# Layer norms transposed by VectorE and a trip through DRAM instead of by TensorE, in a two-layer graph-attention kernel

**Chip, cores, metric.** One core of one Trainium2 chip. The metric is the device time of one execution in microseconds (us), the median of several runs of the built kernel. A ratio is the mean time of one kernel's fast runs over the mean of the other's in the same rounds, so it is not quite the ratio of the medians that stand beside it; its 95% interval follows in brackets.

## The reference, cut to what matters

```python
# x: [64, 256, 512] fp32 (64 batches of 256 nodes), adj: [256, 256]
h = relu(layernorm(x));  x = x + L0(h, adj)      # W: 512x256; softmax over neighbours; concat [out, h W]
h = relu(layernorm(x));  x = x + L1(h, adj)      # q, k, v, o: 512x512 each, with bias; 8 heads of 64, masked softmax
```

Both layers multiply `h` by weights. The kernel's matmuls take `h` with its 512 features on partitions (the axis that the product `h W` sums over), while its layer norms have the nodes on partitions. Each normed 128x512 tile therefore has to be transposed before its product: 4 tiles per group (2 batches) and layer, 256 tiles in all. How this is done is the subject of the change.

## The kernel before

The kernel works by groups of two batches. While TensorE does the attention of group g, it also does the projection (q, k, v) of group g+1 and the first layer of group g+2, piece by piece, in an order that the program fixes. A projection is seven block products in two PSUM banks; each bank is read by ScalarE (`kept`) or VectorE (the additions) before it is accumulated into further. The other engines' orders are chosen when the program is built, except where `after` fixes one.

```python
def after(instruction, name):            # same engine: stand behind `name`; no semaphore is waited for
    tc.add_manual_dep(instruction.ins, name, ...NoSync...)

def norm_T(src, mv, name):               # src [128, 4 tiles, 512]
    ve = small.tile([P, GT], F32, ...);   nc.vector.tensor_scalar(ve, mv[:, :, 1], EPS, None, op0=ALU.add)
    rstd = small.tile([P, GT], F32, ...); nc.gpsimd.tensor_tensor(rstd, ve, rexp, op=ALU.pow)
    def normed(t):
        xn[t] = att.tile([P, D], F32, tag="xn", ..., bufs=2)          # two buffers
        nc.vector.tensor_scalar(xn[t], src[:, t, :], mv[:, t, 0:1], rstd[:, t : t + 1], ...)
    def put(t, dst):
        if t + 1 < GT: normed(t + 1)
        pt = mm(...)                                                   # a PSUM bank
        for c in range(HP): transpose(pt[:, c, :], xn[t][:, c * P : (c + 1) * P], ident)   # TensorE
        nc.scalar.activation(dst, pt, AF.Relu)
    normed(0)
    return put

def operand_sums(quads, sums):            # GpSimd; used for the projection (sums) and for the outputs (o_sums)
    a11, a12, a21, a22 = quads
    nc.gpsimd.tensor_add(sums[:, 0], a21, a22)
    nc.gpsimd.tensor_sub(sums[:, 1], sums[:, 0], a11)
    nc.gpsimd.tensor_sub(sums[:, 2], a11, a21)
    nc.gpsimd.tensor_sub(sums[:, 3], a12, sums[:, 1])

# project(g), for name in q, k, v   (cut to banks and readers)
    def kept(bank, half, i):
        s = att.tile([P, 2, N], F32, tag=f"kept{i}", ..., bufs=1);  take(s, bank, half);  return s
    product(first, 1, True);   p1 = kept(first, 0, 0)
    product(second, 2, True);  nc.vector.tensor_add(part(0, 0), second, p1)
    product(first, 6, False);  p16 = kept(first, 0, 1)
    second = ...               # another bank
    product(second, 7, True);  p7 = kept(second, 1, 2)
    product(first, 5, False);  nc.vector.tensor_add(part(1, 1), first, p7)
    product(second, 4, False); nc.vector.tensor_add(part(1, 0), second, p16)
    product(first, 3, False);  take(part(0, 1), first, 1)   # may start only when the addition from `first` is done

# outputs(g, b): o_sums (GpSimd), seven products of half size, after each: nc.vector.tensor_add(x, out, x)
# weigh(...): attention-weighted sums (pr), reciprocal of the totals, oT; scores(...): sc, exp (ScalarE), mask product (VectorE)
# judge(): a bound on the scores from the weights, checked in small pieces between the others
```

## Time and profile before

| | before |
|---|---|
| time, median of 4 runs (lowest to highest) | 2700.3 us (2698.2 to 2701.9) |
| mean granted TensorE clock | 0.993 |
| busy: TensorE / VectorE / GpSimd / ScalarE | 97 / 62 / 46 / 31% |
| period of a group in mid-kernel | 81.54 us |
| TensorE's waits between 100 and 2600 us | 27 us |

The period is the distance between the same VectorE addition (the first one for `k`) in neighbouring groups, in the timeline. The busy shares, waits, timeline and groups of this kernel are shown in the prediction below.

### The profile page before, as it was taken

Reading aid. Unit: us, or ns where it says so; the run is one execution under the profiler, and the core shown is the slowest. Engines: PE = TensorE matmul, PEld = TensorE weight load, DVE = VectorE, ACT = ScalarE, POOL = GpSimd, SP = SyncE. Lnnn points to the kernel's source line nnn. Section 1 sums busy time; section 2 is a strip of 40 time slices with the busy share of each in tenths; the row PEclk is TensorE's granted clock in tenths of the full one; section 3 lists DMA queues with packets and bytes.
Section 4 is the critical chain, followed back from the end, with each engine's and each line's share of the span. In section 5 each row is a group of like instructions: output and inputs, shape, how many; then the busy total and the mean of one; then the engine's idle time right before and its main releaser. Section 6 shows DMA issues by size and latency. Waiting matters only on the chain.

```text
span 2697.3 us, 41512 instructions
## 1 busy us (share of the span) xinstructions
PE 2620.4 (97%) x17150; PEld 2118.8 (79%) x17150; DVE 1669.7 (62%) x2558; ACT 835.9 (31%) x1771; POOL 1230.0 (46%) x1004
## 2 busy tenths in 40 slices
PE   5999999999999999999999999999999999999997
PEld 3888888878888887887788888788878878878874
DVE  5666566666557665566665576665576656666544
ACT  2333232333332333323333323333333333233321
POOL 2353355443445443545434454435455335445343
PEclk8999999999999999999999999999999999999998
DMA  5000101000001010000000000000000000000000
GB/s 164 1 12 32 36 24 36 13 32 32 28 32 36 9 36 32 24 32 9 32 32 24 32 32 9 32 32 24 32 32 9 32 32 24 32 17 23 17 16 25
DMA packets 45890, 78.49 MB, mean 29 GB/s; under 512 B 3712, under 2 KB 10624, under 8 KB 45696
## 3 DMA queue, kind: packets, MB, share of 16 engines
q1 hardware_dynamic: 45696, 75.77, 8.1%
q8 instruction: 137, 2.24, 0.3%
q14 instruction: 57, 0.47, 0.1%
HBM read 42.21 MB, written 33.55 MB: 28 GB/s over the span
## 4 chain that ended last, share of the span: by engine, by line
PE 89%; DVE 8%; POOL 1%; issue 1%; DMA 0%; ACT 0%; DVEq 0%
PE pq L113 15%; PE pv L113 14%; PE py L113 13%; PE pk L113 13%; PE pr L113 9%; PE ph L113 8%; PE sc L113 7%; PE po L113 4%; PE pt L116 4%; DVE p L573 3%; DVE r L604 2%; PE total L113 2%; DVE k L544 1%; DVE oT L605 1%; PE pn L116 1%
## 5 line engine op out<-in xcount | busy, mean ns | idle before, releaser
L573 DVE TENSOR_TENSOR p<-p,maskT 128x1024 f32<-128x1024 f32 x256 | 398.6, 1588 | 0.6 <-ACT p L572 0.5
L572 ACT ACTIVATE p<-sc 128x512 f32<-128x512 f32 x512 | 264.4, 602 | 380.9 <-PE sc L113 380.9
L574 POOL TENSOR_TENSOR ps<-p 128x512 f32<-128x512 f32 x256 | 366.2, 1447 | 0.0
L628 DVE TENSOR_TENSOR x<-py,x 128x256 f32<-128x256 f32 x448 | 187.6, 419 | 272.8 <-PE py L113 266.9
L604 DVE RECIPROCAL r<-total 128x256 f32<-128x256 f32 x128 | 224.5, 1754 | 194.6 <-PE total L113 194.6
L113 PE MATMUL py<-wo_sb,o_sums 128*128 128x256 f32 x1024 | 266.5, 384 | 26.4 <-DVE x L628 21.6
L420 POOL TENSOR_TENSOR x<-H,x 128x256 f32<-128x256 f32 x128 | 87.7, 685 | 443.0 <-ACT H L419 441.9
L113 PE MATMUL pr<-p,v 128*32 128x256 f32 x4096 | 251.8, 385 | 5.8 <-DVE p L573 5.8
L113 PE MATMUL sc<-q,k 64*128 64x256 f32 x2048 | 255.7, 389 | 0.0
L113 PE MATMUL pq<-sums,wq_sb 128*128 128x256 f32 x1024 | 246.7, 384 | 4.2 <-POOL sums L377 3.7
L113 PE MATMUL ph<-w_sb,hT 128*128 128x258 f32 x1024 | 246.1, 383 | 0.0
L113 PE MATMUL pk<-sums,wk_sb 128*128 128x256 f32 x1024 | 244.8, 382 | 0.0
L113 PE MATMUL pv<-wv_sb,sums 128*128 128x256 f32 x1024 | 242.0, 379 | 0.1
L113 PEld LDWEIGHTS sc<-q,k 64*128 64x128 f32 x2048 | 187.2, 186 | 69.7 <-issue 52.6
L113 PEld LDWEIGHTS py<-wo_sb,o_sums 128*128 128x128 f32 x1024 | 191.2, 192 | 62.9 <-POOL o_sums L377 37.6
L365 ACT ACTIVATE hT<-pt 128x512 f32<-128x512 f32 x256 | 153.1, 599 | 266.0 <-PE pt L116 265.7
L354 DVE TENSOR_SCALAR xn<-x,mv,rstd 128x512 f32<-128x512 f32 x256 | 225.8, 893 | 9.5 <-PE pt L116 4.9
L376 POOL TENSOR_TENSOR o_sums<-oT 128x256 f32<-128x256 f32 x64 | 106.2, 1660 | 262.6 <-DVE oT L605 262.6
L113 PEld LDWEIGHTS pq<-sums,wq_sb 128*128 128x128 f32 x1024 | 190.1, 191 | 39.1 <-issue 9.9
L113 PEld LDWEIGHTS ph<-w_sb,hT 128*128 128x128 f32 x1024 | 195.7, 192 | 28.6
L113 PEld LDWEIGHTS pk<-sums,wk_sb 128*128 128x128 f32 x1024 | 189.3, 190 | 33.9 <-issue 9.9
L113 PEld LDWEIGHTS pr<-p,v 128*32 128x32 f32 x4096 | 121.1, 110 | 112.2 <-issue 39.7
(145 smaller groups left out, 4054.4 us busy)
## 6 DMA issues: line engine op xcount, KB each, us to landing
x<-in_x_dram SPq DMA_DIRECT2D x32, 1024.0 KB, 5.5
out_dram<-x SPq DMA_DIRECT2D x64, 512.0 KB, 2.8
wq_sb<-in_L_gnn_Wq_dram SPq DMA_DIRECT2D x2, 512.0 KB, 11.7
wk_sb<-in_L_gnn_Wk_dram SPq DMA_DIRECT2D x2, 512.0 KB, 12.4
wv_sb<-in_L_gnn_Wv_dram SPq DMA_DIRECT2D x2, 512.0 KB, 11.4
wo_sb<-in_L_gnn_Wo_dram SPq DMA_DIRECT2D x8, 128.0 KB, 3.3
wv_block<-in_L_gnn_Wv_dram SPq DMA_DIRECT2D x4, 256.0 KB, 3.0
wq_block<-in_L_gnn_Wq_dram SPq DMA_DIRECT2D x4, 256.0 KB, 2.9
```

The costliest lines, as they stand in the source:

```text
L113: in_order(nc.tensor.matmul(*args, **kwargs))
L116: in_order(nc.tensor.transpose(*args))
L354: latest[0] = nc.vector.tensor_scalar(xn[t], src[:, t, :], mv[:, t, 0:1], rstd[:, t : t + 1], op0=ALU.subtract, op1=ALU.mult,).ins.name
L365: nc.scalar.activation(dst, pt, AF.Relu)
L376: nc.gpsimd.tensor_add(sums[:, 0], a21, a22)
L420: nc.gpsimd.tensor_add(xt[:, t, F1:], H[:, t, 2 : F1 + 2], xt[:, t, F1:])
L544: nc.vector.tensor_add(part(1, 1), first, p7)
L572: nc.scalar.activation(pair[:, j], sc[j], AF.Exp, scale=scale)
L573: nc.vector.tensor_mul(pair, pair, maskT[:, None, :, :].to_broadcast([P, 2, NT, N]))
L574: nc.gpsimd.tensor_add(ps[:, 2 * i : 2 * i + 2, :], pair[:, :, 0, :], pair[:, :, 1, :])
L604: nc.vector.reciprocal(r, total)
L628: nc.vector.tensor_add(to, out, to)
```

## The change

The intent is to take 248 of the 256 transposes off the engine that sets the time. VectorE transposes each normed tile in 32 by 32 blocks; one transfer per batch writes the result to DRAM and four read it back, each to its 32 partitions (5 transfers per batch and layer); ScalarE's relu then reads SBUF. Group 0 keeps the TensorE form. Norms, loads and stores go by batch. The bound check runs once, near the start. To make room in SBUF, the three `kept` buffers become two of one tag.

```diff
-    def norm_T(src, mv, name): ...          # four tiles at once, each freed by TensorE's transpose
+    def norm_T(src, mv, name, by_pe):
+        def norm(b):                         # one batch: ve, rstd, two xn (tag "xn", bufs=2 as before)
+            ...
+        def turn(b):
+            ...                              # by_pe: as before (group 0)
+            xt = att.tile([P, J, HP, NT, S], F32, tag="xt", ...)
+            moved = att.tile([P, J, HP, NT, S], F32, tag="moved", ...)
+            passed = dram.tile([P, J, HP * NT * S], F32, tag="passed", ...)
+            for t in tiles:
+                nc.vector.transpose(xt[:, :, :, t % NT, :], xn[t].rearrange("p (c j a) -> p j c a", j=J, a=S))
+            nc.sync.dma_start(passed, xt.rearrange("p j c t n -> p j (c t n)"))
+            for j in range(J):
+                nc.sync.dma_start(moved[j * S : (j + 1) * S]..., passed.rearrange("(i a) j e -> j a i e", a=S)[j])
+        def put(b, dst):
+            ... nc.scalar.activation(to, turned[b * NT + t], AF.Relu)
@@ project: kept
-                s = att.tile([P, 2, N], F32, tag=f"kept{i}", name=f"kept{i}_{name}_{g}", bufs=1)
+                s = att.tile([P, 2, N], F32, tag="kept", name=f"kept{i}_{name}_{g}")
@@ first_layer (the second layer likewise: norm(0) at r == 2, turn(0) at r == 3, then norm(1), turn(1))
-        put = norm_T(xt, mv, f"0_{g}")
-        yield GAP
+        norm(0);  yield GAP
+        turn(0);  norm(1);  yield GAP
+        turn(1);  yield GAP;  yield GAP
+        put(0, hT[0]);  yield GAP
@@ main loop (cut: loads and stores by batch; the check's products in fewer, larger pieces)
-    verdict = judge()          # ahead of the main loop, its pieces spread over the groups
+    verdict = judge()          # ahead of group 0, its pieces within the start
```

## The prediction

> **What bounds the kernel now.** I began with the busy shares and the slices of the page.
>
> ```profile
> PE 2620.4 (97%) x17150; PEld 2118.8 (79%) x17150; DVE 1669.7 (62%) x2558; ACT 835.9 (31%) x1771; POOL 1230.0 (46%) x1004
> ...
> PE   5999999999999999999999999999999999999997
> ...
> PEclk8999999999999999999999999999999999999998
> ```
>
> TensorE is busy 97% at full clock, in every slice but the first and the last. No other engine passes 62%. A busy TensorE may still hide slack, so I next read its waits between 100 and 2600 us.
>
> ```profile
> PE py L113 <- DVE x L628: 20.7, 26, 1.0
> PE pt L116 <- DVE xn L354: 5.1, 2, 2.9
> PE py L113 <- DVE part L292: 0.6, 1, 0.6
> PE pq L113 <- DVE q L544: 0.5, 1, 0.5
> ```
>
> They add up to 27 us of 2500: the middle of the kernel is one unbroken stream of matmuls, and its time is the sum of their steps. So a block of PE work is worth what it moves the start of the next one. The timeline of TensorE in one group of two batches shows that step:
>
> ```profile
> 1413.28 1.89 PE L113 MATMUL pv<-wv_sb,sums 128*128 128x256 f32 x8
> 1415.01 0.60 PE L116 MATMUL pt<-ident,xn 128*128 128x128 f32 x4
> 1415.45 1.89 PE L113 MATMUL pv<-wv_sb,sums 128*128 128x256 f32 x8
> 1417.18 0.60 PE L116 MATMUL pt<-ident,xn 128*128 128x128 f32 x4
> 1417.61 1.89 PE L113 MATMUL pv<-wv_sb,sums 128*128 128x256 f32 x8
> ```
>
> A pt block (the four transposes of one 128x512 tile) starts at 1415.01 and the next matmul at 1415.45: 0.44 us, although it is drawn 0.60 us long. From 1417.18 to 1417.61 it is 0.43. The groups give the count, and the durations that I use for the engines that take the work over:
>
> ```profile
> L354 DVE TENSOR_SCALAR xn<-x,mv,rstd 128x512 f32<-128x512 f32 x256 | 225.8, 893 | 9.5 <-PE pt L116 4.9
> ...
> L340 DVE BATCH_NORM_STATS2 st<-x 128x6 f32<-128x512 f32 x256 | 169.1, 680 | 15.8 <-DMA x<-in_x_dram 4.9
> L116 PE MATMUL pt<-ident,xn 128*128 128x128 f32 x1024 | 156.2, 276 | 10.6 <-DVE xn L354 10.6
> ```
>
> 1024 transposes are 256 blocks, eight in each of 32 groups. The chain of waits gives pt 4% of the span (some 108 us), the same size.
>
> [...]0.435 / 4 is 0.109 us a transpose, since they overlap. I use the step. [...]680 ns for the statistics of 128x512, 692 ns for a 128x512 tensor product. For fp32 this is my least certain duration. [...]the trace has 5.5 us for the 1 MB load of x and 2.8 us for the 512 KB store of out, so I use the trace's.
>
> **The change part by part.**
>
> *TensorE loses 248 blocks.* Group 0 keeps its eight. 248 x 0.435 us = 107.9 us, all on the path. A group's period falls from 81.55 us (DVE L534 k at 1379.84 and again at 1461.38) by 8 x 0.435 = 3.48 to 78.07 us.
>
> *VectorE gains 248 transposes.* 248 x 0.69 = 171 us (5.5 a group). Its total becomes 1670 + 171 = 1840, or 71% of 2600. Beside the path, if they fall in its gaps.
>
> *ScalarE keeps 256 relus*, 599 ns each, now out of SBUF instead of PSUM. No change counted. PSUM loses a user (pt), which can only help.
>
> *DMA gains 124 trips* (31 groups, two layers, two batches): 512 KB out, then four reads of 128 KB. That is 124 x 1 MB = 130 MB over 2600 us, 50 GB/s beside the present 29; the first slice moved 164 GB/s. Bandwidth is no issue. Latency: write 2.8 us, four issues of 0.37 us each 1.5, last read 3.3 us (the eight wo_sb loads have the same 128 KB on 32 partitions), first issue 0.4: about 8 us from the transposes to the relu.
>
> *The bound check moves to the start.* Its matmuls (gram 2 x 32, square 2 x 24, at 0.108 us) cost 12 us, spread today over the PE-bound part. In the first 80 us TensorE was busy only 48, so perhaps half is hidden there: minus 6. Its twelve extra block loads go, and so does the 2.92 us for which pt waited on xn behind the check's small tests: minus 4 with its other stalls.
>
> **Does the 8 us fit?** The tightest place is the second layer's last batch, whose operand sums the next group's projection needs. PE order is fixed by the program. From the trace of before (PE times of the group at 1405): scores end at 1409.7; seven products of 1.73 follow without pt blocks, to 1421.8; then weights and scores 4.2, and 2 products and 3 half-size output blocks (6.1) before the first product with the sums that need this batch (the third of the projection), at 1432.1. On VectorE the last statistics end at 1408.3; reciprocal, oT and the two mask products (1.7 + 0.7 + 3.2) have earlier places, then two norms (1.8) and two transposes (1.4): 1417.1. Plus 8 us is 1425, two relus 1426.2, two POOL sums of 1.3 us 1428.8. Slack 3.3 us. The first layer's transposes depend on x that was loaded long before, so their slack is at least that. Hence I expect no regular wait, but not much to spare: I add 10 us (0.3 a group) for more waits on a busier VectorE, of the kind of py waiting for x, and 3 us at the start, where group 1's trips have only seven projection steps to hide in.
>
> Sum: 2701.5 - 107.9 - 6 - 4 + 10 + 3 = 2596.6; I say 2600, leaning to the late side.
>
> **Rivals.**
>
> *A. The trip is not hidden.* ScalarE and VectorE run in a fixed order. If a relu stands in ScalarE's queue ahead of the copies and exponentials, and its data comes late, everything behind waits. For it: only two projection steps (3.5 us) lie between the last turn and its relu in the program; SyncE issues in order, so a store or load that waits there can hold a read back; the write must land before the reads start. Against it: the other engines' order isn't program order (in the trace the b_out additions run at 1413.88, ahead of the sums at 1424.01 that the program has first), ScalarE is idle 69%, and the slack above is 3.3 us. A trip of 14 us instead of 8 would cost about 2.7 us a group, 31 x 2.7 = 84 us: some 2685, within 2%.
>
> *B. VectorE becomes the bound.* If an fp32 transpose takes twice as long (1.4 us), VectorE adds 347 us: 2017 of 2600, 78%. Still under TensorE, but the present wait of py for x (0.8 us a group) could grow to 2: some 2640. Against it: its gaps in that group, of 8.2, 4.3, 3.9, 3.2 and 2.3 us in its timeline, can take 5.5 us more.
>
> *C. The transposes were hidden anyway*, so that little is gained: 0.60 us drawn, some of it overlapped. The measured step of 0.435 speaks against it; it is already the part not overlapped. Under this rival, 2690.
>
> *D. The check's move helps more*: 12 + 4 us and no new waits, 2578.
>
> **Range and chances.** D gives the lower end, 2575. B and a mild A (1 us a group more) give 2630 to 2640; with the uncertainty of the trip I set the upper end at 2655. Faster by over 2% means under 2647.5: A in full, or C, must hold for it to fail. I give these together 0.15: faster 0.85, same 0.13, slower 0.02 (the last needs waits of over 5 us a group).
>
> **What would show it.** Right: pt x32 left on TensorE; about 2510 us of PE busy time; a DVE transpose of 128x512 near 0.69 us, 248 times; write to last read near 8 us; a group period near 78.3 us; PE's waits in the middle below 45 us; the check's matmuls all in the first 110 us. Wrong: PE waiting for POOL sums, ACT hT or the trips' DMA in every group; a transpose above 1 us. The prediction fails most easily through the trip: if it takes over 11 us from transpose to relu, each us more is 31 us of time.

## More of the kernel before

One more line of its page is used, that of the chain of work that ended last:

```profile
PE 89%; DVE 8%; POOL 1%; issue 1%; DMA 0%; ACT 0%; DVEq 0%
```

Followed back from the end of the kernel, 89% of the span is TensorE working.

## The result

The changed kernel takes **2907.8 us** (2904.5 to 2908.6, 4 runs), ratio **1.0767 [1.0748, 1.0785]**: slower by 7.7% where 3.8% faster was predicted. The granted clock is 0.959. The page of the changed kernel, lines as in the one of before:

```profile
PE 2609.9 (90%) x16158; PEld 2050.9 (71%) x16158; DVE 1751.3 (60%) x2847; ACT 823.3 (28%) x1759; POOL 1257.8 (43%) x1072
...
PE   6889988899888899888998888998889988889997
...
PE 51%; DVE 33%; POOL 11%; issue 4%; DMA 0%; ACT 0%; SPq 0%; DVEq 0%; POOLq 0%; ACTq 0%
```

992 matmul instructions are gone (17150 - 16158 = 4 x 248), as planned, but TensorE falls below 90% in 25 of the 40 slices, where it was below in two, and a third of the chain is now VectorE, 11% GpSimd. VectorE is *less* busy in share (60%) than before: it is not saturated, it is in the way. TensorE's waits between 100 and 2800 us (columns: total us, times, longest) name where:

```profile
PE pv L114 <- DVE v L585: 144.2, 30, 4.9
PE pq L114 <- POOL sums L399: 56.3, 30, 8.2
PE py L114 <- DVE x L671: 25.4, 30, 0.8
PE pv L114 <- ACT kept_v L555: 23.8, 29, 0.8
```

Before it was 27 us (100 to 2600), 21 of it of the third kind. Now it is 252. The largest wait comes once per group: product 3 of v's projection waits for the addition `part(1, 1)` that reads its bank. The three stalls in one group, in TensorE's timeline:

```profile
1436.73 1.99 PE L114 MATMUL pv<-wv_sb,hT 128*128 128x256 f32 x8 [0.82 <-ACT kept_v L555]
1443.63 3.78 PE L114 MATMUL pv<-wv_sb,sums 128*128 128x256 f32 x8 [4.91 <-DVE v L585]
...
1460.30 1.99 PE L114 MATMUL pq<-sums,wq_sb 128*128 128x256 f32 x8 [1.66 <-POOL sums L399]
```

Why was that addition late? VectorE's timeline of the changed kernel, from v's first addition (L575) to the awaited one (L585):

```profile
1435.35 0.65 DVE L575 TENSOR_TENSOR v<-pv,kept_v 128x512 f32<-128x512 f32 x1
1435.93 0.61 DVE L350 TENSOR_SCALAR ve<-mv 128x2 f32<-128x2 f32 x1
1437.36 1.00 DVE L356 TENSOR_SCALAR xn<-x,mv,rstd 128x512 f32<-128x512 f32 x2 [0.82 <-POOL rstd L352]
1438.28 1.30 DVE L376 STREAM_TRANSPOSE xt<-xn 128x512 f32<-128x512 f32 x2
1439.50 1.24 DVE L338 BATCH_NORM_STATS2 st<-x 128x6 f32<-128x512 f32 x2
...
1440.99 0.17 DVE L350 TENSOR_SCALAR ve<-mv 128x2 f32<-128x2 f32 x1
1441.98 1.00 DVE L356 TENSOR_SCALAR xn<-x,mv,rstd 128x512 f32<-128x512 f32 x2 [0.82 <-POOL rstd L352]
1442.89 0.68 DVE L585 TENSOR_TENSOR v<-pv,kept_v 128x512 f32<-128x512 f32 x1
```

The same stretch in the kernel before (L534 and L544 are the same two additions):

```profile
1417.69 0.65 DVE L534 TENSOR_TENSOR v<-pv,kept_v 128x512 f32<-128x512 f32 x1
...
1418.73 0.99 DVE L354 TENSOR_SCALAR xn<-x,mv,rstd 128x512 f32<-128x512 f32 x2
1419.64 0.68 DVE L544 TENSOR_TENSOR v<-pv,kept_v 128x512 f32<-128x512 f32 x1
```

Between the additions lay 1.95 us from start to start; now 7.54 us. In between stand the four norms of a later group's first layer (two lines of two), each pair with its `ve` and a wait of 0.82 us for GpSimd's `rstd`, and also two transposes and two statistics. None of that is urgent: that layer's first product (`ph`) starts at 1475.19, 38 us after these norms. The addition that TensorE waits for starts only when all of it is done.

The stall was also paid for afterwards. Three stretches of the changed kernel, before it, over it and after it (columns: us, TensorE busy with its count, **granted clock**, DMA share, GB/s):

```profile
1400.00:1436.00 36.00, 35.05 (x235) 1.00 0.17 59
1436.00:1444.00 8.00, 2.36 (x9) 0.88 0.59 192
1444.00:1450.00 6.00, 6.00 (x44) 0.59 0.63 183
```

In the 6 us after the stall the clock is 0.59; asked for in steps of 1 us, it is 0.50 from 1443 to 1448 and 1.00 again from 1449. The block of eight pv matmuls at 1443.63 took 3.78 us against 1.89 for the same block before (shown in the prediction), and over the kernel the groups pv<-sums and pr<-p,v grew from 242.0 to 286.4 and from 251.8 to 273.6 us busy: 66 us.

Finally the two pieces that I had priced, in the groups (busy us, mean ns) and the DMA view (KB each, median us to landing):

```profile
L376 DVE STREAM_TRANSPOSE xt<-xn 128x512 f32<-128x512 f32 x248 | 163.5, 687 | 0.0
```

```profile
passed<-xt SPq DMA_DIRECT2D x124, 512.0 KB, 2.8
moved<-passed SPq DMA_DIRECT2D x496, 128.0 KB, 3.5
```

A transpose is 687 ns, with 675 for the statistics of the same size (predicted 690, an estimate from the 680 ns of the statistics and the 692 ns of a product of that size in the trace of before), the write 2.8 us (2.8), a read 3.5 (3.3). Nothing that was added was clearly dearer than predicted.

**The sum.** The period is 88.75 us (1308.38, 1397.12, 1485.87) where 78.07 was predicted: 10.7 more. Of it the v wait is 144.2/30 = 4.8, the one for `sums` without its first (56.3 - 8.2)/29 = 1.7, `kept_v` 0.8, the clock 6 x (1 - 0.59) = 2.5 (66 / 30 = 2.2 by the busy times). About 0.9 us is not split further. Over the span the waits grew by 225 us and the clock cost 66, against 108 saved: 183 of the 207 us, the rest is not split.

### The profile page after: what moved, and what is told of

The parts are those of the page before. It is cut to its first block, busy times and chain, and to the rows that moved or that the text cites.

```text
span 2905.7 us, 40980 instructions
## 1 busy us (share of the span) xinstructions
PE 2609.9 (90%) x16158; PEld 2050.9 (71%) x16158; DVE 1751.3 (60%) x2847; ACT 823.3 (28%) x1759; POOL 1257.8 (43%) x1072
## 4 chain that ended last, share of the span: by engine, by line
PE 51%; DVE 33%; POOL 11%; issue 4%; DMA 0%; ACT 0%; SPq 0%; DVEq 0%; POOLq 0%; ACTq 0%
PE pq L114 10%; PE pk L114 9%; PE ph L114 8%; PE pr L114 7%; PE py L114 6%; DVE p L614 6%; DVE r L645 6%; DVE st L338 5%; DVE xn L356 4%; PE pv L114 4%; DVE xt L376 3%; POOL rstd L352 2%; POOL sums L398 2%; PE sc L114 2%; PE po L114 2%
## 5 line engine op out<-in xcount | busy, mean ns | idle before, releaser
L114 PE MATMUL pv<-wv_sb,sums 128*128 128x256 f32 x1024 | 286.4, 441 | 144.2 <-DVE v L585 144.2
L614 DVE TENSOR_TENSOR p<-p,maskT 128x1024 f32<-128x1024 f32 x256 | 387.2, 1544 | 21.9 <-ACT p L613 21.7
L114 PEld LDWEIGHTS pv<-wv_sb,sums 128*128 128x128 f32 x1024 | 223.4, 222 | 192.4 <-DVE v L585 156.2
L398 POOL TENSOR_TENSOR o_sums<-oT 128x256 f32<-128x256 f32 x64 | 76.5, 1195 | 586.2 <-DVE oT L646 586.2
L114 PE MATMUL pr<-p,v 128*32 128x256 f32 x4096 | 273.6, 411 | 6.0 <-DVE p L614 6.0
L352 POOL TENSOR_TENSOR rstd<-ve,rexp 128x2 f32<-128x2 f32 x128 | 91.3, 713 | 430.8 <-DVE ve L350 290.9
L114 PEld LDWEIGHTS pr<-p,v 128*32 128x32 f32 x4096 | 127.4, 118 | 142.2 <-issue 78.5
L356 DVE TENSOR_SCALAR xn<-x,mv,rstd 128x512 f32<-128x512 f32 x256 | 176.3, 711 | 77.2 <-POOL rstd L352 76.3
L400 POOL TENSOR_TENSOR o_sums<-oT 128x256 f32<-128x256 f32 x64 | 100.9, 1576 | 278.1 <-DVE oT L646 276.5
```

Of the source, the lines that this page charges most:

```text
L114: in_order(nc.tensor.matmul(*args, **kwargs))
L356: latest[0] = nc.vector.tensor_scalar(xn[r], src[r], mv[:, r, 0:1], rstd[:, t : t + 1], op0=ALU.subtract, op1=ALU.mult,).ins.name
L614: nc.vector.tensor_mul(pair, pair, maskT[:, None, :, :].to_broadcast([P, 2, NT, N]))
```

## The experiments

Theories that I set out with. **T1, order:** the late addition is a matter of place in VectorE's order, and so are the smaller waits. **T2, buffers:** two `kept` buffers instead of three hold the projection up. **T3, load:** VectorE's 164 us more work and 130 MB of transfers slow everything. The kernel before ran beside, at 2699.2 to 2699.5 us median. All outputs are right.

| run | what | us | ratio to before | clock |
|---|---|---|---|---|
| after | the change | 2907.8 | 1.0767 | 0.959 |
| e2_p7place | one kept buffer less needed | 2908.5 | 1.0772 | 0.959 |
| e4_before_kept2 | before, with two kept buffers | 2700.1 | 1.0002 | 0.993 |
| e8_before_with_trip | before, with unread transposes and trips | 2729.4 | 1.0107 | 0.990 |
| e1_order | v's additions ahead of the norms | 2721.0 | 1.0078 | 0.986 |
| e3_order_p7 | e1 and e2 | 2734.4 | 1.0124 | 0.980 |
| e9_two_orders_only | e1 and a GpSimd order | 2645.2 | 0.9795 | 0.992 |
| e5_pool_order | e3 and the GpSimd order | **2636.8** | **0.9762** | 0.993 |
| e6_norms_behind_masks | norms elsewhere | 2807.0 | 1.0399 | 0.958 |
| e7_po_earlier | e6, `po` steps earlier | 2827.8 | 1.0474 | 0.954 |
| e10_xn_behind_masks | only xn elsewhere | 2719.8 | 1.0078 | 0.995 |
| e11_stats_then_xn | e10, statistics late too | 2677.0 | 0.9918 | 0.993 |
| e12_trip_longer | e11 with a longer trip | 2822.2 | 1.0455 | 0.961 |

### e1_order: the awaited addition first

```diff
-            nc.vector.tensor_scalar(ve, mv[:, tiles, 1], EPS, None, op0=ALU.add)
+            first = nc.vector.tensor_scalar(ve, mv[:, tiles, 1], EPS, None, op0=ALU.add)
+            if name[0] == "0" and added[0] is not None:      # first layer only
+                after(first, added[0])
...
-            nc.vector.tensor_add(part(1, 0), second, p16)
+            added[0] = nc.vector.tensor_add(part(1, 0), second, p16).ins.name
```

No instruction, buffer or transfer is changed, and VectorE gets no new semaphore wait; only its order.

> The changed kernel with one thing more: VectorE's norms of the next group's first layer are ordered behind the last addition of v's projection (an order on VectorE alone, no new wait between engines). Theory T1 (the new place of these norms in VectorE's fixed order, ahead of the addition that TensorE waits for, is the cause): TensorE's wait of pv for the addition of v (144 us, 4.8 us in each group) falls under 20 us, the granted clock rises from 0.96 to about 0.99, and the time comes to 2600 to 2660 us. Theory T2 (two buffers for the kept copies in place of three are the cause): the wait only moves, 2850 to 2910 us. Theory T3 (the longer way through DRAM is the cause): 2800 us or more, with waits for the sums in place of those for v.

Measured: 2720.97 us (2716.79 to 2723.15), ratio 1.0078 [1.0061, 1.0095]. The large wait is gone, and another has grown:

```profile
PE py L114 <- POOL o_sums L401: 68.5, 30, 3.4
...
PE pv L114 <- DVE v L588: 1.8, 1, 1.8
```

187 of the 208 us come back from the place of one small instruction, a batch's `ve`. The additions L578 and L588 are 1.97 us apart again (1428.57 and 1430.54), with the two statistics still between them, and the norms and transposes follow. The wait for `sums` goes too (one of 8.2 us is left), so in the changed kernel it followed from the late addition. The time missed the 2600 to 2660 us of T1, since TensorE now runs into GpSimd's order.

### e2_p7place: one kept buffer less

```diff
-            p7 = kept(second, 1, 2)
+            p7 = part(1, 1)
+            take(p7, second, 1)          # kept copy in place, where the sum goes anyway
```

> The changed kernel, but the third kept copy (of product 7) goes straight into its place in q, k or v and is added to there, so that it no longer waits for a buffer. T1: the 24 us wait of pv for the copy goes (0.8 us a group), but the addition of v still stands behind the norms on VectorE, which do not move, so TensorE waits that much longer for it: 2880 to 2910 us. T2: most of the loss goes, 2650 us or less.

Measured: 2908.49 us, ratio 1.0772 [1.0754, 1.079]. The wait for `kept_v` (22.9 us between 100 and 2600 us) vanished, that for v's addition grew from 139.2 to 169.8 in the same stretch: TensorE only came earlier to the same late addition. So the `kept_v` wait was hidden behind the larger one.

### e3_order_p7: both

> Both edits. T1: a little under the run with the order alone, by at most the 24 us of the copies' wait: 2580 to 2640 us. T3: 2800 us or more.

Measured: 2734.4 us (2730.95 to 2738.1), ratio 1.0124 [1.0107, 1.0141]: 13 us *slower* than e1, a miss. TensorE, 24 us earlier by the missing `kept_v` waits, waits longer for `o_sums` (80.8 us, 12 more) and for v's additions (14.0, 12 more), and the longer stalls (up to 3.9 us) go with a lower clock (0.980 against 0.986). What GpSimd does at such a stall:

```profile
1364.40 1.27 POOL L400 TENSOR_TENSOR sums<-hT 128x512 f32<-128x512 f32 x1 [3.65 <-ACT hT L394]
1365.62 1.28 POOL L402 TENSOR_TENSOR sums<-hT 128x512 f32<-128x512 f32 x1
1366.86 2.25 POOL L401 TENSOR_TENSOR sums<-sums,hT 128x512 f32<-128x512 f32 x1
1369.07 1.70 POOL L400 TENSOR_TENSOR o_sums<-oT 128x256 f32<-128x256 f32 x1
1370.74 1.26 POOL L403 TENSOR_TENSOR sums<-hT,sums 128x512 f32<-128x512 f32 x1
1371.96 0.72 POOL L401 TENSOR_TENSOR o_sums<-o_sums,oT 128x256 f32<-128x256 f32 x1
```

The outputs' two sums, for which TensorE waits until 1372.73 (a stall of 2.47 us), stand behind and between the projection's four. Their input `oT` is ready at 1366.63 on VectorE; what then holds them up is the sum at 1366.86 (2.25 us) and the one at 1370.74 (1.26). It is the same illness on a second engine.

### e4_before_kept2: the buffers in the kernel before

```diff
-                s = att.tile([P, 2, N], F32, tag=f"kept{i}", name=f"kept{i}_{name}_{g}", bufs=1)
+                s = att.tile([P, 2, N], F32, tag="kept", name=f"kept{i}_{name}_{g}")
```

> The kernel before with two buffers for the kept copies in place of three and nothing else; the order of VectorE's instructions stays as it was. T1: within 1% of the kernel before, at most 24 us more. T2: slower by 100 us or more.

Measured: 2700.1 us (12 runs), ratio 1.0002 [0.9993, 1.0011]. With e2, T2 has fallen: the fewer buffers are neither necessary nor sufficient for the loss.

### e8_before_with_trip: the load without the use

The kernel before, with every transpose and trip of the change carried out beside TensorE's own, the results unread. To make room, the kept copies are put in place and the check's squares into PSUM.

```diff
+            nc.vector.transpose(xt[:, :, :, t % NT, :], xn[t].rearrange("p (c j a) -> p j c a", j=J, a=S))
+            if t % 2:
+                nc.sync.dma_start(passed, xt.rearrange("p j c t n -> p j (c t n)"))
+                for j in range(J): nc.sync.dma_start(moved[j * S : (j + 1) * S]..., passed...[j])
```

> The kernel before, which still transposes on TensorE, and beside it all that the change adds: the 248 VectorE transposes, each batch's 512 KB to DRAM and the four transfers back to SBUF, where nobody reads them (the kept copies go straight to their places and the bound check's squares to PSUM, to make room). Theory T1: VectorE's 170 us and the transfers are harmless by themselves, within 1.5% of the kernel before (under 2740 us). Rival (VectorE's load or the transfers cost the time): 2780 us or more.

Measured: 2729.39 us, ratio 1.0107 [1.0091, 1.0124]. 13.5 of the 30 us is one wait for the moved squares, a side effect of the edit; another 13.0 us, over 26 times, is `pt` waiting for `xn` (5.1 before). Load and transfers alone cost little, so T3 explains at most a small part. TensorE has no wait for v's additions at all in it; in this kernel its own transposes still decide when an `xn` buffer is free, which I take for the reason.

### e5_pool_order and e9_two_orders_only: GpSimd's order too

```diff
-        operand_sums(quads, sums)                 # all four at once
+        operand_sums(quads, sums, 0)              # first two at once
...      # in project, ahead of product 6 of q, the first that needs them:
+            third = operand_sums(quads, sums, 1)  # third and fourth
+            after(third, summed[0])               # behind the outputs' first two sums (None is skipped)
```

e5 is e3 with this. e9 is e1 with this, that is, the change with orders fixed on two engines and nothing else.

> The run with both edits (order and kept copy in place, 2734 us), and on GpSimd the two sums of the outputs that TensorE asks for first are ordered ahead of the third and fourth sum of the next group's operands. Theory U1 (what is left after the VectorE order is GpSimd's fixed order: the outputs' sums stand behind operand sums that wait for the data from DRAM): the wait of py for the outputs' sums (81 us, some 2.5 us a group) falls to 50 us or less, 2690 to 2715 us. Theory U2 (the sums are late only because the data from DRAM are late): the wait moves from py to pq and the time stays within 10 us of 2734.

> The changed kernel with the two orders alone (VectorE's norms behind v's additions, GpSimd's outputs' sums ahead of the third and fourth operand sum); the kept copies stay in two buffers. If the two orders are the whole cause: within 25 us (the 24 us that pv waits for the copy) of the run that has the copy in place as well (2637 us), so 2630 to 2665 us.

Measured: e5 **2636.82 us** (2633.79 to 2639.07), ratio **0.9762 [0.9746, 0.9778]**; e9 2645.19 (2643.62 to 2646.61), 0.9795 [0.9779, 0.9811]. The `o_sums` wait falls from 80.8 us (e3) to 18.8 in e5:

```profile
PE py L114 <- POOL o_sums L404: 18.8, 26, 2.1
```

It did not move to `pq`, as theory U2 had it: `pq` waits for `sums` once, 8.2 us. The clock is back at 0.993 and 0.992, and that is why e5 beat its expectation (2690 to 2715 us), which counted the wait alone: 62 us of the 98 gained are the wait, and the rise from 0.980 to 0.993 is worth some 35 of 2700. e9 came as expected (2630 to 2665). The periods are 79.20 and 79.62 us. Fixing two orders turns 7.7% slower into 2.05% faster (by its interval, 1.9 to 2.2%); with the kept copy in place, 2.4% faster. e5 is the fastest kernel. Mind how p7 in place cost 13 us in e3 and gained 8 in e5: a wait is only worth removing where no later one takes it up.

### e6_norms_behind_masks and e7_po_earlier: another place for the norms

Could the norms go where VectorE has more room, behind the mask products of the current attention step?

```diff
+        masked[0] = nc.vector.tensor_mul(pair, pair, maskT...).ins.name      # in scores
...      # first layer's bn_stats and ve:
+        after(instruction, masked[0])
```

e6 has this on e5's GpSimd order and kept copy in place (without e1's order); e7 has one main-loop step changed besides, `"uosoosuosoosuos"` to `"uososusosuosooo"`, so that the layer's results come earlier.

> The changed kernel with three edits: all of the next group's first-layer statistics and norms stand on VectorE behind the mask products of the step that issues them (later than in the run with the order alone), the third kept copy in its place, and GpSimd's order as in the run before. VectorE then reaches the second layer's transposes 1.3 us earlier (two statistics less ahead of them) and the outputs' sums get their input earlier. U1: waits of TensorE in the middle under 80 us, 2620 to 2690 us.

> The same, and in the third step of each group the first layer's output products (po) stand two to three half-size output blocks (0.87 us each) earlier in TensorE's order, so that norms, transposes and the way through DRAM start earlier against TensorE's stream. If lateness of that chain is what is left: 30 to 60 us less than the run without it; if VectorE's fullness in that step is the limit: within 15 us of it.

Measured: e6 2807.02 us, ratio 1.0399 [1.0381, 1.0416]; e7 2827.81, 1.0474 [1.0456, 1.0491]. Both far off. VectorE in e6:

```profile
1409.67 1.00 DVE L356 TENSOR_SCALAR xn<-x,mv,rstd 128x512 f32<-128x512 f32 x2 [4.37 <-POOL rstd L352]
```

It reaches `xn` early and stands idle 4.37 us for GpSimd's `rstd`, which comes at 1408.93 behind the operand sums and two `ps` additions; behind it on VectorE stand, from 1410.59, the additions of the outputs, and TensorE stalls 4.22 us for their bank. In all, `py` waits 143.0 us for x, with the clock at 0.958, nearly the sizes of the changed kernel's v wait and clock. This is the order mechanism produced in another place, though I had not meant to: nearly the same stall length, the same clock. e7 is 21 us slower than e6, outside both of its expectations; as its edit moved the output blocks too, it shows only that earlier steps do not help here.

### e10_xn_behind_masks and e11_stats_then_xn: taking the idle wait out

```diff
+        after(xn, masked[0])                      # (both condensed) e10: the norms alone, first layer
+        after(bn_stats, added[0]); after(ve, added[0])     # e11: besides, statistics behind v's additions
```

Both have e5's GpSimd order and the kept copy in place; e10 has no order behind v's additions.

> Copy in place, GpSimd's order, and only the first layer's normalizations (xn) stand behind the mask products; their statistics and rstd run early as in the changed kernel. GpSimd's rstd then is done long before VectorE comes to xn, so the 4.4 us for which VectorE stood at xn in the run with norms and statistics behind the masks goes: 2610 to 2650 us. If VectorE's fullness there is itself the limit: 2750 us or more, as in that run.

> As the run before, with the first layer's statistics behind v's additions as well. It takes the two statistics (1.3 us) from in front of the second layer's transposes and of v's addition: waits of TensorE in the middle under 50 us, 2600 to 2635 us, the fastest of all.

Measured: e10 2719.76 us, ratio 1.0078 [1.0061, 1.0095]; e11 2677.04, 0.9918 [0.9901, 0.9934]. Both miss (2610 to 2650 and 2600 to 2635). The long stall is gone, as intended; what stays are some 118 short waits of `py` for x, 90 us. In e11 the norms between the outputs' additions are slow:

```profile
1395.23 1.00 DVE L356 TENSOR_SCALAR xn<-x,mv,rstd 128x512 f32<-128x512 f32 x2 [0.83 <-POOL rstd L352]
...
1416.01 2.35 DVE L356 TENSOR_SCALAR xn<-x,mv,rstd 128x512 f32<-128x512 f32 x2
```

The same pair of norms takes 1.00 us at 1395.23, when GpSimd is idle until 1395.86, most of that time, and 2.35 us at 1416.01, when it adds sums without a break from 1413.37 to 1424. The two durations go with what GpSimd does meanwhile; why, no run isolates.

e10 serves the clock question as well: 90.5 us of waits for x and 36.1 for v, none longer than 1.8 us (apart from one of 6.1 for the first sums), and a granted clock of 0.995 (0.993 in the kernel before): with stalls of that length it was no lower here. Between them and the 4.91 us it is mixed. In e3 the first four `py` matmuls after a stall for `o_sums` took 1.13 us behind one of 2.47 us (at 1372.73) and 2.08 us behind one of 2.46 us in the next group (at 1454.15). e1, whose `o_sums` stalls reach 3.4 us, has a clock of 0.986.

### e12_trip_longer: how much slack has the trip?

```diff
+            again = dram.tile([P, J, HP * NT * S], F32, tag="again", ...)
+            nc.sync.dma_start(again, passed)          # one more copy, DRAM to DRAM
...
-                    passed.rearrange("(i a) j e -> j a i e", a=S)[j],
+                    again.rearrange("(i a) j e -> j a i e", a=S)[j],
```

> That kernel with the way through DRAM made longer: each batch is copied once more from DRAM to DRAM (an estimate of 3 us, from the 2.8 us of the 512 KB store). If the 8 us way has 2 us or less to spare: 30 to 60 us slower. If it has more to spare: within 15 us.

Measured: 2822.19 us, ratio 1.0455 [1.0438, 1.0473], against 2677.04 of e11: 145 us slower, outside both expectations. The copy takes 4.3 us, the period grows from 80.92 to 85.34, by 4.4, and TensorE now waits for the projection's sums:

```profile
PE pq L114 <- POOL sums L404: 143.3, 29, 7.2
```

It looks as if the trip had no slack left, but the traces say otherwise. In e11 the awaited second sum ends at 1417.21 (L402 at 1414.97, 2.24 us) and its product starts at 1419.78, so 2.6 us are to spare. In e12 the relu ends at 1407.10 (1405.95, 1.15 us), and GpSimd then does this:

```profile
1408.05 2.67 POOL L636 TENSOR_TENSOR ps<-p 128x512 f32<-128x512 f32 x2
1410.69 1.44 POOL L403 TENSOR_TENSOR sums<-hT 128x512 f32<-128x512 f32 x1
1412.09 1.45 POOL L405 TENSOR_TENSOR sums<-hT 128x512 f32<-128x512 f32 x1
1413.50 1.26 POOL L404 TENSOR_TENSOR sums<-sums,hT 128x512 f32<-128x512 f32 x1
```

TensorE waits 4.86 us for the last of these. Ahead of it stand two `ps` additions and the third sum, 4.1 us together by their durations; in e11 both come behind it. The build with the longer trip has another order on GpSimd, so e12 changes two things, and most of this wait can be the order's. Some 2.6 us of slack is what e11 shows; what a longer trip costs by itself stays open.

## Why the prediction was wrong, by its own steps

- **What bounds the kernel** was right: TensorE's unbroken stream.
- **TensorE loses 248 blocks, 107.9 us, period 78.07.** Right (the old period, there 81.55, is 81.54). e5's period of 79.20 less its new waits per group, (18.8 + 14.1)/30 = 1.1, is 78.1.
- **VectorE gains 171 us.** Right in size (163.5), and VectorE isn't the bound (60%): rival B is dead. "Beside the path, if they fall in its gaps" is the condition that did not hold, and I did not follow it up.
- **DMA trips, 8 us.** Right in its parts; in e3 a write starting at 1356.01 was followed by the end of the wait for its relu at 1363.17. The slack, estimated at 3.3 us, is 2.6 in e11. That each us of a longer trip costs 31 was not tested: e12 changed an order too.
- **The check's move, minus 10 us; the start, 3.** No run separates them, but the traces show the start: the first scores begin at 114.88 before, 117.25 in the changed kernel and 118.58 in e5, although the check's 12 us of matmuls now lie ahead of them. Behind that point, the next projection waits 8.2 us for its sums, once, so the 3 was too small. e5's 2637 against 2597 predicted is 31 x (79.20 - 78.07) = 35 us of period and some 5 us of such ends.
- **The step that failed** is "Does the 8 us fit?", with its end: "I add 10 us (0.3 a group) for more waits on a busier VectorE". Measured: waits of 225 us more, plus 66 us of clock, some 9.4 us a group instead of 0.3; and TensorE waited for GpSimd's sums in every group, which the prediction had named as a sign of being wrong. I followed one thing through the pipeline, the second layer's data on its way to TensorE, and took the orders of VectorE and GpSimd from the trace of before, as if the change left them alone. It rewrote them. The first layer's norms and transposes I dismissed with "their slack is at least that": true of when *they* are needed, and beside the point, for the question is whom they stand in front of.
- **What put them there** I infer from code and orders: before, `xn` has two buffers, each freed by TensorE's transpose, so a group's norms could only be done one by one as TensorE went along, with v's additions in between. When VectorE itself frees them, four norms can be done in one stretch, and they were placed early, although in both programs they are issued after the v additions that they now precede. e1, which moves them back by order alone, shows that the place is the cause; why it was chosen stays argued, with e8 in its favour.
- **Rival A** said that fixed orders of ScalarE and VectorE could hold work back and came nearest, but it charged ScalarE's late relu, at 2.7 us a group. The runs show VectorE's norms at 4.8 and, following from them, GpSimd's sums at 1.7. The relus are not ahead of ScalarE's copies but behind: the one at 1452.12 follows v's copy, which stood 10.78 us waiting for the stalled TensorE, and an exponential. SyncE's order did hold reads back, as A said it could: a write issued at 1346.64 landed 2.6 us later, at 1349.24, but its reads were issued from 1351.28 on, after a second write that had waited 3.8 us for its transposes. **Rivals C and D** are out: the transposes did cost TensorE time, and the check isn't the size of what happened.
- **The clock** was in no step. I had read 0.993 as given. It is a term that the long stalls added here: none to be seen where the regular stalls were 1.8 us or less (e10, clock 0.995), 2.2 to 2.5 us a group where they were 4.9 (clock 0.959).

## What to carry to other kernels

When work is taken off the engine that sets the time, ask what its back-pressure was holding back: buffers that it used to free now come free early, and non-urgent work can move up in the orders of the other engines. A new instruction's price is its place, not its share of a half-idle engine: look, in each engine's order, at what now stands ahead of the instructions that the bound engine waits for, and fix the order explicitly (here orders on two engines, worth 263 us: 187 on VectorE, e1, and 76 on GpSimd, e9 against e1). Judge each removed wait by where the next one lies, and avoid few long stalls more than many short ones, since here the long ones were paid again in clock (0.959 with one of up to 4.9 us in each group, 0.995 in e10). And look at the orders again after every edit, the test edits included (e12).
